# One ring of row tiles, tables with alternating ranks, deviations by logarithm and exponential, and a new order of steps in a graph attention kernel

## The chip, the cores and the metric

The kernel runs on one core of a Trainium2 chip. The metric is the device time of one execution in microseconds (us); for several executions the median is given. The core has a matrix engine (TensorE, PE in the profile), a vector engine (VectorE, DVE), an engine for activation functions (ScalarE, ACT), a general one (GpSimd, POOL) and a queue engine (SyncE, SP). Transfers between the memory of the chip and the on-chip memory run on DMA engines, and are started by SP, ACT and POOL.

## What is computed

`x` has 32 batches of 512 rows (channels) by 1024 columns (nodes); `adj` is 512 by 512. Two layers follow each other, each on a layer norm of the rows with a ReLU:

```python
h = jnp.maximum(_layernorm(x, axis=-1), 0.0)
q = jnp.einsum('c,bcn->bn', wq, h)
k = jnp.einsum('c,bcn->bn', wk, h)
scores = q[:, None, :] + k[:, :, None]
scores = jnp.where(scores > 0, scores, 0.01 * scores)
att = softmax(scores, axis=-1)
agg = jnp.einsum('bcn,bmn->bcm', h, att)
x = x + relu(jnp.einsum('oc,bcm->bom', adj, agg) + bm[None, :, None])

h = jnp.maximum(_layernorm(x, axis=-1), 0.0)
W = adj * adj
x = x + jnp.einsum('bnf,nm->bmf', h, W) + bias
```

The attention has 1024 by 1024 scores per batch, each a leaky ReLU of a sum of two numbers. For a fixed node m, the sum q[n] + k[m] is positive for all n whose q lies above -k[m] and negative for the others. If the nodes are sorted by q, then the softmax of a node is made of two parts: a sum over the nodes of high rank with weights exp(q), and a sum over those of low rank with weights exp(0.01 q). So prefix sums over the sorted values, from both ends, replace the 1024 by 1024 matrix.

## The kernel before

**One batch.** A batch has 4 tiles of 128 channels by 1024 nodes (2 MB in all). `load` brings the tiles, `stats` (VectorE) makes mean and variance of each row, `norm` (ScalarE) the standard deviation, `slopes` (VectorE) its reciprocal, and `relu` (ScalarE) normalises in place. `scores` (TensorE) makes q and k in pieces of 256 nodes, `copy` brings them to the on-chip memory, and they go to a small table in the chip's memory and back as `row` (q of all nodes, on every partition). `columns` turns q and k so that each node has a partition (8 groups of 128 nodes). `factors` works out the maximum of q and the factors of a node.

**Ranks.** `rank` (VectorE) counts for each node how many q lie below its own; `lower` (ScalarE, a sign with a sum) counts how many lie below -k. `to_rows` and `from_rows` turn the two counts into row numbers of a table. `value` (TensorE, 32 matmuls of 128 by 512) multiplies h by the transposed adjacency, `spread` (ScalarE) copies the result out, and `scatter` (GpSimd, an indirect DMA of 128 rows) writes the values, 512 numbers and the node's q, into the rank's row of the table.

**Scan.** A table has 9 blocks of 126 ranks in 63 pairs. `fetch` (SP) reads a sorted table back in three pieces of three blocks; `weights` (ScalarE) makes the exponentials, `later`, `totals` and `stationary` (VectorE, TensorE, GpSimd) the triangular matrices, and `scan` (TensorE) the prefix sums, block after block, from both ends. Since the first row of each block takes what the block before it has summed, `sums` (ScalarE) copies one row into the next block, and copies the sums out, and SP writes them into the table, beside the sorted values: each row s of a table is three entries long (k = 0, 1, 2), of which `scan` fills 0 and 1 and `scatter` entry 2.

**Back.** `gather` (GpSimd, 8 indirect DMAs of 128 rows of three entries) reads for every node the two sums and the value at the border between them. `excess`, `divide`, `weigh` and `combine` (VectorE, ScalarE) make of them the attention's result. `turn` (TensorE) transposes it to channels by nodes and VectorE adds it to the tile that `reload` has read again from `x`. Then the second layer: `stats`, `norm`, `slopes`, `relu` into tiles of their own, `lift` (adds the bias), `propagate` (TensorE, 8 groups of 4 matmuls of 128 by 512) and `finish` (VectorE), which starts the write to `out` after a tile's second half.

**The order of the work.** There are no loops over batches in the usual sense. Each function is a step with a planned time in the dictionary `PLAN` (one for each call in a batch, in a unit of its own); a batch's steps stand `T = 80.647` later than the previous batch's. `FIRST` and `LAST` give the first five and the last five batches a shift, and a stretch about the mean of a step's times. `plan` puts all into one list, which is sorted by time and emitted once:

```python
t = s.b * T + t + shift + stretch * (t - mean)
...
steps.sort(key=lambda e: e[:2])
with tc.manual_schedule():
```

So the numbers set nothing but an order. Each engine executes its instructions in this order and each waits for what it needs; a step that stands early on its queue and waits holds up what stands behind it. SP's queue carries the loads, reloads, fetches, sums and outputs; ACT's the small table of q; POOL's the scatters and gathers. A batch lasts about five of these periods from load to output, so that several are in flight.

**Memory.** The tiles of 128 by 1024 come from three pools: `xp` (7 tiles), `yp` (7) and `hp` (4, the second layer's h). `load`, `reload` and `relu` choose between them. A pool hands out its tiles in turn, and one that is still read delays the step that wants it. The tables `td` are five in the chip's memory (`TABLES`), the batch number modulo five chooses one; `qd` are two. The values of a gather have one buffer (`gp`), the sorted blocks five (`vsp`), the scattered values eight (`vp`).

**Set-up.** Four small loads (`wq`, `wk`, `bm`, `bias`) and the adjacency; `turn_adjacency` transposes it on TensorE and `square` squares it on GpSimd. `pads` fills the rows of the tables that no rank has (zero, with q at -1e30), for all tables in one step.

Of the kernel before, what the change touches and what calls it, by code (L numbers as in the profile page):

```python
# [16 lines left out]
P = 128  # L17
# [8 lines left out]
TABLES = 5  # L26
PLAN = {
    "adjacency": (-108.2,),
    "biases": (103.637,),
    "columns": (-0.644,),  # L30
    "combine": (
        295.175, 296.981, 297.681, 298.56, 293.456, 294.898, 296.312, 299.441, 298.758,
        299.991, 297.356, 298.478, 299.289, 299.451, 296.18, 297.782,
    ),
    "compare_mask": (-39.924,),
    "divide": (279.776,),
    "excess": (274.084,),
    "factors": (31.052,),
    "fetch": (71.51,),
    "finish": (356.071, 361.635, 372.571, 377.123, 391.802, 417.732, 398.837, 420.531),  # L40
    "from_rows": (87.236,),
    "gather": (260.35, 264.453, 263.071, 264.447, 267.501, 263.458, 263.983, 262.344),
    "later": (82.669,),
    "lift": (343.707, 352.288, 361.264, 350.629),
    "load0": (-132.547,),
    "load1": (-83.561,),
    "load2": (-110.642,),
    "load3": (-58.45,),
    "lower": (25.135, 20.956, 15.44, 19.087, 14.733, 13.756, 46.166, 37.237),
    "masks": (-18.987,),  # L50
    "norm0": (-31.509,),
    "norm1": (326.35,),
    "pads": (-73.925,),
    "propagate": (346.423, 349.207, 352.169, 365.765, 371.233, 382.761, 381.981, 389.706),
    "rank": (17.984, 18.872, 20.129, 19.992, 25.594, 25.16, 26.367, 26.318),
    "reload0": (283.236,),
    "reload1": (289.947,),
    "reload2": (275.592,),
    "reload3": (294.126,),
    "relu0": (-21.389, -21.25, -20.652, -20.617),  # L60
    "relu1": (336.308, 336.463, 336.836, 338.53),
    "row": (1.149,),
    "scan": (88.672, 94.082, 102.974, 119.344, 135.342, 151.67, 171.394, 183.726, 197.836),
    "scatter": (49.236, 49.927, 49.759, 49.383, 53.226, 50.436, 50.301, 52.611),
    "scores": (-2.312,),
    "slopes0": (-23.106,),
    "slopes1": (327.104,),
    "spread": (10.418, 15.798, 4.081, 13.981, 26.765, 25.953, 18.654, 18.733),
    "square": (58.25,),
    "stationary": (82.87, 113.617, 158.362),  # L70
    "stats0": (-66.042, -57.278, -62.987, -37.25),
# [725 lines left out]
```

## Time and profile before

| | |
|---|---|
| median of 3 runs | 2368.5 us (2366.38 to 2370.43) |
| span of the profiled execution | 2372.9 us |
| mean granted TensorE clock | 0.987 of full speed |
| moved by DMA | 643.45 MB, mean 271 GB/s |
| VectorE's statistics | 256 of 677 ns in layer 0, 256 of 668 ns in layer 1 |
| ScalarE's ReLU, layer 0 | 128 of 1231 ns |
| scatter, gather on GpSimd | 256 of 1064 ns, 256 of 951 ns |

The profile is of one execution. Its page gives each engine's busy time, the span in 40 slices with busy tenths (9 is 90% or more) and the granted TensorE clock, the DMA queues, the chain of work that ended last, and groups of instructions (source line L, engine, operation, result<-operands, count, mean duration). The trace behind it can be asked for the chain in order of time (start, length, engine, what), for an engine's instructions with the idle time ahead of them, and for the busy time of every engine in a given stretch. In these answers `pv` is the value product, `pg` the propagate product, `sc` a scan, `tr` a turn, `pq` scores, `pr` columns, `pd` totals, `td` a table, `vs` a sorted piece, `g` the gathered rows, `h` the second layer's normalised tiles.

### The profile page before, as it was taken

The numbers are of one execution on the slowest core, as the hardware profiler recorded it, in microseconds if no ns is written. First come the engines' busy times: TensorE is split into PE (matmuls) and PEld (weight loads), VectorE is DVE, ScalarE is ACT, GpSimd is POOL, SyncE is SP. The second block draws the span as 40 slices with busy tenths as digits, with TensorE's granted clock in tenths as the row PEclk, the third lists the DMA queues.
The fourth block names the chain that finished last, engine by engine and source line by source line (L and its number), as shares of the span: only waits on it lengthen the run. The fifth ranks groups of instructions, "written<-read, shape, count | busy, mean of one in ns | idle before, by whom it ended". The sixth has DMA issues, their size and how long they took to land.

```text
span 2372.9 us, 28069 instructions
## 1 busy us (share of the span) xinstructions
PE 2295.2 (97%) x7568; PEld 1011.5 (43%) x7568; DVE 1952.6 (82%) x5008; ACT 1599.8 (67%) x2880; POOL 720.7 (30%) x973
## 2 busy tenths in 40 slices
PE   7787999999999999999999999999999999999997
PEld 3233444444444444444444444444444444443443
DVE  7457888888888888888888888888888888888875
ACT  4576776766777766777676777676677676677551
POOL 2233333233333233233223233323333323233310
PEclk9988999999999999999999999999999999999998
DMA  6678888989999998999999999899988898998972
GB/s 222 171 181 277 284 284 277 296 269 276 287 290 285 296 286 266 277 299 283 288 292 266 276 294 287 287 291 272 268 291 276 288 302 253 276 282 269 311 294 79
DMA packets 206894, 643.45 MB, mean 271 GB/s; under 512 B 29120, under 2 KB 29248, under 8 KB 206736
## 3 DMA queue, kind: packets, MB, share of 16 engines
q1 hardware_dynamic: 142944, 355.74, 53.9%
q0 software_dynamic: 57344, 268.99, 30.7%
q10 hardware_dynamic: 6448, 16.92, 2.3%
q8 instruction: 61, 1.00, 0.2%
q14 instruction: 97, 0.79, 0.1%
HBM read 429.94 MB, written 211.60 MB: 270 GB/s over the span
## 4 chain that ended last, share of the span: by engine, by line
PE 85%; DMA 5%; DVE 5%; ACT 2%; issue 1%; POOL 1%; SPq 0%; ACTq 0%; another core or an unknown queue 0%; POOLq 0%; DVEq 0%
PE pg L703 34%; PE pv L550 33%; PE sc L639 10%; PE tr L696 4%; DMA vs<-td 2%; PE pq L445 2%; PE sc L636 1%; DVE g L689 1%; DVE st L414 1%; DMA g<-td,idg 1%; DMA td<-v,idx 1%; DVE junk L492 1%; ACT x L433 0%; DVE junk L487 0%; DMA x<-in_x_dram 0%
## 5 line engine op out<-in xcount | busy, mean ns | idle before, releaser
L703 PE MATMUL pg<-h,wsq 128*128 128x512 f32 x2048 | 911.2, 598 | 12.8 <-ACT h L433 12.8
L550 PE MATMUL pv<-wmT,x 128*128 128x512 f32 x2048 | 908.8, 598 | 5.9 <-ACT x L433 4.4
L703 PEld LDWEIGHTS pg<-h,wsq 128*128 128x128 f32 x2048 | 382.8, 191 | 517.4 <-issue 476.1
L550 PEld LDWEIGHTS pv<-wmT,x 128*128 128x128 f32 x2048 | 382.0, 191 | 499.1 <-issue 452.6
L623 POOL TENSOR_TENSOR sm<-mask_a,wc 128x192 f32<-128x192 f32 x96 | 51.9, 540 | 1254.9 <-DVE wc L600 785.7
L689 DVE SCALAR_TENSOR_TENSOR g<-g,cf 128x512 f32<-128x512 f32 x512 | 357.9, 756 | 46.4 <-ACT g L685 44.3
L648 ACT COPY vs<-sc 1x512 f32<-1x512 f32 x256 | 145.3, 567 | 272.9 <-PE sc L639 208.6
L563 POOL DMA_INDIRECT td<-v,idx x256 | 272.4, 1064 | 149.3 <-POOL v L562 36.3
L639 PE MATMUL sc<-vs,sm 128*64 128x512 f32 x1024 | 282.6, 621 | 21.3 <-POOL sm L623 11.1
L503 ACT ACTIVATE junk<-qrow,qk 128x1024 bf16<-128x1024 f32 x256 | 294.0, 1148 | 5.5 <-DMA qrow<-qd 2.5
L660 POOL DMA_INDIRECT g<-td,idg x256 | 243.5, 951 | 147.4 <-issue 71.5
L698 DVE SCALAR_TENSOR_TENSOR y<-tr,nbm,y 128x512 f32<-128x512 f32 x256 | 174.4, 744 | 66.3 <-PE tr L696 61.2
L711 DVE SCALAR_TENSOR_TENSOR y<-pg,bm_sb,y 128x512 f32<-128x512 f32 x256 | 185.8, 731 | 32.4 <-PE pg L703 32.0
L651 ACT COPY t<-sc 128x512 f32<-128x512 f32 x288 | 168.0, 583 | 40.7 <-DMA td<-t 35.3
L433 ACT ACTIVATE x<-x,nmr,rstd 128x1024 f32<-128x1024 f32 x128 | 148.6, 1231 | 64.9 <-DVE nmr L425 64.9
L492 DVE TENSOR_SCALAR_CACHE_REDUCE junk<-qrow,qk,cnt 128x896 bf16<-128x896 f32 (+6 forms) x224 | 180.5, 806 | 8.2
L685 ACT ACTIVATE g<-g,cf 128x512 f32<-128x512 f32 x256 | 167.7, 712 | 6.4 <-DVE cf L679 5.3
L487 DVE TENSOR_SCALAR_CACHE_REDUCE junk<-qrow,qk 128x128 bf16<-128x128 f32 (+6 forms) x224 | 166.0, 741 | 6.6
L414 DVE BATCH_NORM_STATS2 st<-x 128x6 f32<-128x512 f32 x256 | 162.7, 677 | 9.6 <-DMA x<-in_x_dram 9.6
L439 DVE TENSOR_TENSOR y<-y,bias_sb 128x1024 f32<-128x1024 f32 x128 | 154.3, 1219 | 16.0 <-ACT h L433 16.0
L557 ACT COPY v<-pv 128x512 f32<-128x512 f32 x256 | 141.8, 579 | 29.7 <-PE pv L550 14.0
L414 DVE BATCH_NORM_STATS2 st<-y 128x6 f32<-128x512 f32 x256 | 160.4, 668 | 0.0
(111 smaller groups left out, 1923.1 us busy)
## 6 DMA issues: line engine op xcount, KB each, us to landing
vs<-td SPq DMA_DIRECT2D x192, 384.8 KB
td<-t SPq DMA_DIRECT2D x576, 128.2 KB
x<-in_x_dram SPq DMA_DIRECT2D x128, 512.0 KB
y<-in_x_dram SPq DMA_DIRECT2D x128, 512.0 KB
out_dram<-y SPq DMA_DIRECT2D x128, 512.0 KB
qrow<-qd ACTq DMA_DIRECT2D x32, 512.0 KB
td<-v,idx POOLq DMA_INDIRECT x256, 8.3
g<-td,idg POOLq DMA_INDIRECT x256, 13.8
```

The lines of the kernel that those rows point to most:

```text
L414: nc.vector.bn_stats(st[:, i, :], s.x[c][:, ts(i, HALF)])
L492: nc.vector.tensor_scalar(junk[:, j * P :], s.qrow[:, j * P :], qc, first, ALU.is_lt, ALU.add, accum_out=s.cnt[:, 1, j : j + 1],)
L503: nc.scalar.activation(junk, s.qrow, AF.Sign, bias=s.qk[:, 1, j : j + 1], accum_out=s.sgn[:, j : j + 1])
L550: nc.tensor.matmul(pv, s.h[c][:, ts(j, P)], wmT[:, c, :], start=(c == 0), stop=(c == NC - 1))
L563: i = nc.gpsimd.indirect_dma_start(tds[s.b % TABLES][:, :], bass.IndirectOffsetOnAxis(ap=s.idx[j // 4][:, j % 4 : j % 4 + 1], axis=0), v[: ...
L639: nc.tensor.matmul(p[ts(k, HP), :], m[:, k, :], s.vs[h][:, 0:C], start=True, stop=True)
L651: nc.scalar.copy(t[:, 0:C], p)
L660: nc.gpsimd.indirect_dma_start(s.g[:, j, :], None, tds[s.b % TABLES][0 : 3 * NB * HP, :].rearrange("(s k) w -> s (k w)", k=3), bass.Indire ...
L689: nc.vector.scalar_tensor_tensor(r, s.g[:, j, k * W : k * W + C], s.cf[:, k, j : j + 1], r, ALU.mult, ALU.add)
L698: nc.vector.scalar_tensor_tensor(xh, pt, nbm[:, o : o + 1], xh, ALU.max, ALU.add)
L703: nc.tensor.matmul(pg, wsq[:, r, ts(c, P)], s.h[r][:, ts(i, HALF)], start=(r == 0), stop=(r == NC - 1),)
L711: nc.vector.scalar_tensor_tensor(xh, s.pg.pop((c, i)), bm_sb[:, c : c + 1], xh, ALU.add, ALU.add)
```

## The change

1. The pools `xp`, `yp` and `hp` become one ring of 18 tiles (`ROWS`), and `load`, `reload` and `relu` take the next tile of it without a choice.
2. There are six tables instead of five, and four small tables for q instead of two (`QROWS`).
3. The layout of a table changes. Before, even ranks stood in the first half of the table and odd ranks in the second, 64 rows for each block. Now each block has 128 rows, even ranks in the first 64 and odd ranks in the last 64. So `fetch` reads three blocks as one transfer over 128 partitions instead of two over 64, and `to_rows`, `from_rows`, `sums` and `gather` reckon the row numbers anew; `from_rows` has one small VectorE operation more. `gather` now has the whole table as its source. A new step, `holes`, one for each table, fills entries 0 and 1 of the rows of odd ranks with zeros (2.36 MB each: 64 rows of 9 blocks of 1026 numbers), by a fill on GpSimd and a transfer on SP. `pads` is a step for each table, with three transfers instead of four.
4. `norm` no longer takes a square root. It takes the logarithm of the variance plus epsilon and the exponential of minus half of that, and `slopes` improves this with one Newton step of three small VectorE operations in place of the reciprocal. The table of activation functions is chosen once at the start.
5. All numbers of `PLAN`, `FIRST` and `LAST` are new, with the same period `T`; `FIRST` and `LAST` have six batches each instead of five, and nearly every stretch is now different from zero.

```diff
-TABLES = 5
+TABLES = 6
+ROWS = 18
+QROWS = 4
 PLAN = {
...
-    "fetch": (71.51,),
+    "fetch": (55.702,),
...
-    "load0": (-132.547,),
-    "load1": (-83.561,),
-    "load2": (-110.642,),
-    "load3": (-58.45,),
+    "load0": (-118.054,),
+    "load1": (-95.975,),
+    "load2": (-139.732,),
+    "load3": (-67.716,),
...
-    "scores": (-2.312,),
+    "scores": (-17.953,),
...
-    "turn0": (305.575, 305.673, 305.631, 305.894),
+    "turn0": (289.134, 289.42, 289.067, 289.284),
...
 FIRST = {
...
     "rank": (
-        (-28.589, 0.7379), (-2.87, -0.0721), (-9.055, 1.3394), (2.403, 0.1874), (-13.459, 0.0458),
...
+        (-34.203, 1.1418), (-6.053, 1.4966), (-21.016, 1.0747), (1.116, -0.688), (10.257, 0.0895),
+        (-0.536, -1.144),
+    ),
...
-    xp = ctx.enter_context(tc.tile_pool(name="xp", bufs=7))
-    yp = ctx.enter_context(tc.tile_pool(name="yp", bufs=7))
-    hp = ctx.enter_context(tc.tile_pool(name="hp", bufs=NC))
+    xp = ctx.enter_context(tc.tile_pool(name="xp", bufs=ROWS))
...
     def sorted_rows(td, h, n):
-        rows = td.rearrange("(o h s k) w -> o s h k w", o=2, s=HP, k=3)
-        return rows[:, :, h : h + n, 2, :]
+        rows = td.rearrange("(h p k) w -> p h k w", p=P, k=3)
+        return rows[:, h : h + n, 2, :]
...
-    root = const.tile([P, 1], F32, name="root")
-    nc.scalar.activation(root, eps_sb, AF.Sqrt)
+    nc.scalar.preload_act_table_set("natural_log_exp_and_others")
...
-    def pads(s):
-        pad = vp.tile([P, W], F32, tag="v", name="pad")
+    def pads(s, i):
+        pad = vp.tile([P, W], F32, tag="v", name=f"pad_{i}")
         nc.vector.memset(pad, 0.0)
         nc.vector.memset(pad[:, C : C + 1], FAR)
-        for td in tds:
-            for o in range(2):
-                nc.sync.dma_start(sorted_rows(td, 0, NB - 1)[o, 0], pad[0 : NB - 1, :])
-                nc.sync.dma_start(sorted_rows(td, NB - 1, 1)[o, :, 0], pad[0:HP, :])
+        for o in range(2):
+            nc.sync.dma_start(sorted_rows(tds[i], 0, NB - 1)[o * HP], pad[0 : NB - 1, :])
+        nc.sync.dma_start(sorted_rows(tds[i], NB - 1, 1)[:, 0], pad)
+
+    def holes(s, i):
+        rows = tds[i].rearrange("(h o s k) w -> o s h (k w)", o=2, s=HP, k=3)
+        z = vsp.tile([P, 3, W], F32, tag="vs", name=f"z_{i}").rearrange("p k w -> p (k w)")
+        nc.gpsimd.memset(z[0:HP, 0 : 2 * W], 0.0)
+        nc.sync.dma_start(
+            rows[1, :, :, 0 : 2 * W],
+            z[0:HP, 0 : 2 * W].unsqueeze(1).broadcast_to([HP, NB, 2 * W]),
+        )
...
     def load(s, c):
-        pool, tag = (yp, "y") if NC <= s.b * NC + c < NC + 7 else (xp, "x")
-        t = pool.tile([P, N], F32, tag=tag, name=f"x_{s.b}_{c}")
+        t = xp.tile([P, N], F32, tag="x", name=f"x_{s.b}_{c}")
...
-        nc.scalar.activation(s.std, s.mv[:, :, 1], AF.Sqrt, bias=eps_sb)
+        nc.scalar.activation(s.std, s.mv[:, :, 1], AF.Ln, bias=eps_sb)
+        s.rstd = sp.tile([P, NC], F32, tag=f"rstd{layer}", name=f"rstd{layer}_{s.b}")
+        nc.scalar.activation(s.rstd, s.std, AF.Exp, scale=-0.5)
...
     def slopes(s, layer):
-        s.rstd = sp.tile([P, NC], F32, tag=f"rstd{layer}", name=f"rstd{layer}_{s.b}")
-        nc.vector.reciprocal(s.rstd, s.std)
+        t = sp.tile([P, NC], F32, tag=f"step{layer}", name=f"step{layer}_{s.b}")
+        nc.vector.scalar_tensor_tensor(t, s.mv[:, :, 1], EPS, s.rstd, ALU.add, ALU.mult)
+        nc.vector.scalar_tensor_tensor(t, t, -0.5, s.rstd, ALU.mult, ALU.mult)
+        nc.vector.scalar_tensor_tensor(s.rstd, t, 1.5, s.rstd, ALU.add, ALU.mult)
...
         if layer == 1:
-            pool, tag = (xp, "x") if s.b == B - 2 else (hp, "h")
-            h = pool.tile([P, N], F32, tag=tag, name=f"h_{s.b}_{c}")
+            h = xp.tile([P, N], F32, tag="x", name=f"h_{s.b}_{c}")
...
-        odd = 3.0 * NB * HP
+        odd = 3.0 * HP
...
-        nc.vector.scalar_tensor_tensor(s.idg, pair, 1.0, block, ALU.add, ALU.add)
+        nc.vector.tensor_scalar(block, block, float(P - PAIRS), 1.0, ALU.mult, ALU.add)
+        nc.vector.tensor_tensor(s.idg, pair, block, ALU.add)
...
-            for o in range(2):
-                d = nc.sync.dma_start(t[ts(o, HP)], sorted_rows(tds[s.b % TABLES], 3 * i, 3)[o])
-                for k in s.sc:
-                    tc.add_manual_dep(d.ins, k.name, DONE, reason="any of them may hold a row")
+            d = nc.sync.dma_start(t, sorted_rows(tds[s.b % TABLES], 3 * i, 3))
+            for k in s.sc:
+                tc.add_manual_dep(d.ins, k.name, DONE, reason="any of them may hold a row")
...
-        nc.sync.dma_start(td[ts(ha, HP), 0, :], t[0:HP, :])
-        nc.sync.dma_start(td[ts(hb, HP), 1, :], t[HP:P, :])
+        nc.sync.dma_start(td[ts(2 * ha, HP), 0, :], t[0:HP, :])
+        nc.sync.dma_start(td[ts(2 * hb, HP), 1, :], t[HP:P, :])
...
-            tds[s.b % TABLES][0 : 3 * NB * HP, :].rearrange("(s k) w -> s (k w)", k=3),
+            tds[s.b % TABLES].rearrange("(s k) w -> s (k w)", k=3),
```

## The prediction

> **What bounds the kernel now.** I read the page's busy shares and slices first, then the chain of waits, then busy time by stretch, then the chain again in the first 262 us, last TensorE's own timeline at the end.
>
> ```profile
> span 2372.9 us, 28069 instructions
> PE 2295.2 (97%) x7568; PEld 1011.5 (43%) x7568; DVE 1952.6 (82%) x5008; ACT 1599.8 (67%) x2880; POOL 720.7 (30%) x973
> PE   7787999999999999999999999999999999999997
> DMA  6678888989999998999999999899988898998972
> ```
>
> The first four slices (240 us) and the last are the only ones in which PE is not full. The chain of waits over the whole span:
>
> ```profile
> 525.43 17.36 PE pv L550 x40
> ...
> 595.96 17.36 PE pv L550 x40
> ...
> 666.48 17.36 PE pv L550 x40
> ```
>
> The same piece returns every 70.53 us, batch after batch: the middle is PE's own work and nothing else. 32 x 70.53 = 2257 of 2373 us; some 116 us are filling and draining. By stretch (columns: length, then busy us of PE, PEld, DVE, ACT, POOL; granted clock, DMA share, GB/s):
>
> ```profile
> 0.00:60.00 60.00, 44.54 (x163) 19.13 (x164) 43.20 (x132) 29.46 (x44) 15.43 (x29) 1.00 0.70 221
> 60.00:120.00 60.00, 47.20 (x146) 18.09 (x145) 26.71 (x92) 35.01 (x72) 13.27 (x24) 0.95 0.67 172
> 120.00:180.00 60.00, 53.46 (x168) 21.45 (x165) 32.06 (x110) 42.01 (x84) 19.17 (x29) 0.91 0.74 185
> 180.00:240.00 60.00, 42.16 (x157) 19.19 (x155) 41.48 (x121) 40.33 (x79) 19.01 (x25) 0.86 0.85 265
> 480.00:900.00 420.00, 420.00 (x1410) 186.64 (x1409) 363.10 (x930) 296.92 (x536) 133.38 (x177) 1.00 0.92 283
> ```
>
> PE idles 52.6 us in the first 240, and its clock falls after the waits. What it waits for, from the chain of the first 262 us:
>
> ```profile
> 96.79 7.00 DMA td<-v,idx
> ...
> 107.26 9.96 DMA vs<-td
> ...
> 180.13 16.16 DMA g<-td,idg
> ...
> 224.42 11.12 DMA vs<-td
> ```
>
> Each early batch goes rank, scatter to the table, fetch, weights, scan in series. At the end (PE's timeline, idle time in brackets):
>
> ```profile
> 2141.28 0.44 PE L461 MATMUL pr<-ident,qr 128*128 128x128 f32 x2 [2.53 <-ACT qr L450]
> ...
> 2212.05 0.28 PE L612 MATMUL pd<-w,mask_a 128*64 128x9 f32 x2 [2.12 <-ACT w L589]
> ...
> 2337.72 30.41 PE L703 MATMUL pg<-h,wsq 128*128 128x512 f32 x64 [10.29 <-ACT h L433]
> ```
>
> **The Trainium skill.** "ScalarE: Activation LUTs", What ACT_TABLE_LOAD costs, puts a table load at 1283 ns; the trace agrees (61 at std, 28, 27 and 6 at the exponentials, 1283 ns each). Its Table sets section says that one set holds both exponential and logarithm; the built program has one load left. "TensorE: Matmul & The Clock Gate", The HAM clock gate: an idle PE restarts at half clock. The trace agrees: four scan matmuls take 2.43 us after the 4.39 us wait at 118.58, and 1.08 warm. "DMA: Bandwidth & Descriptors", Issuing engines are not separate DMA queues: all transfers share 16 engines, so the new zero fills compete with whatever flies beside them; most that I see here is 405 GB/s (10 to 15 us).
>
> **The change, part by part.**
> *Table loads.* 122 x 1.283 = 157 us leave ACT, 64 exponentials x 0.30 = 19 come. DVE gets per norm three products for one reciprocal (+2 x 0.17) and one more small operation in from_rows: +0.85 us per batch. In the middle both are hidden under PE: per 70.53 us DVE has 9.5 us free, ACT 20. Worth 0 there; without that cover it would be -4.3 and +0.85 us per batch.
> *One ring.* 7 + 7 + 4 tiles become 18: the same memory. PE's work per batch is untouched (same 4336 matmuls). *Fetch* is 3 transfers instead of 6 of the same bytes: 3 x 0.62 us of SP issue less in each batch's chain.
> *New times, middle.* In the built order a batch still turns three batches, propagates four batches behind its scores. From excess to the turn DVE has about 25 us (lifts, two statistics, factors, divide, 16 combines of 0.70) under 27 us of PE work; the gathers follow stationary0 as before (8.4 us into the period), so land before excess. I take 0; a stall of 0.1 us per batch would cost 3.
> *New times, start.* This is the cost. SP now issues first the adjacency (1 MB), three pads and a tile of the third batch; the first batch's last two tiles stand behind the wait for the bias vector. Such waits for small loads held SP to 9.82 and 13.35 us in the trace, at the second batch's tiles; now they meet the first batch. I take issue at 12 us and 4 us to land: first statistics at 16 (4.78 before). Then 4 x 1.45, pad and masks on DVE, two activations and four small products: 24.5; four relus 4.64 and the last three score groups: scores end at 32 (17.96 before). The row of q came 6.5 us later; now it flies beside three zero fills of 2.36 MB (7.1 MB, 17.5 us of all engines at 405 GB/s), so 6.5 to 14; I take 9.5: 42 (24.9 before). A rank costs 538.8/256 = 2.10 us; eight, two pad fills, factors (1.9) and one to_rows (1.4): first scatter at 64, eight at 1.46 and a fill on POOL: last at 77 (49.5 before). Fetch 3.5 later, weights 12 after that: 92.5, against 67.5.
> Second batch: its ranks stand on DVE behind those weights, after two statistics (3.0); last scatter 30 us later, fetch 6.5, landing 12.5, weights 1.3: 142 (117.6). Third: only five ranks are left behind (10.5 + 3.0 + 1.4), eight scatters, then the same: 188 (170). Then stationary0 and, queued behind it on POOL, the first batch's gathers: 1.3 + 25.1 (171.35 to 196.41), and 16.4 of excess, divide, weigh and combine: the first turn at 231 (214.15).
> PE has 145.6 us of work in front of that turn (146.5 before), so it runs 85.5 us behind its work, against 67.6. But before, it went on losing, to 76.1 at the first propagate (263.34, 187.2 us of work in front), since the fourth batch's scan waited; now that scan comes at about 252, when PE gets there. Loss: 86 - 76 = **+10**, bounds +1 (bias vector at 8 us, row at 6.5, faster fetch) to +18.
> *New times, end.* The copy of q now stands ahead of the previous batch's weights on ACT, and PE has 7 us of work between scores and columns instead of 3.5: the 2.53 and the cold restart behind it (1.7) go. The last fetch starts with three issues and the last totals wait about 1 instead of 2.4. With the one gather buffer, turns chain: from the 29th batch's turn to the end of the 30th's took 44.0 us, since one of eight gathers stood behind stationary0 of the last batch, itself behind its weights; now all eight go first, 10.3 issue, 14 landing, 2 divide, 13 to combine, turn: 40.3. The two later links stay 39 and 45. Sum -4.2 - 0.3 - 3.7 = **-8**, bounds -12 and -3.
> *Last chain.* Logarithm, exponential and three products in the last norm for square root and reciprocal, all bare: +0.30 + 0.05 + 2 x 0.19 = **+0.7**. The table loads there were already hidden.
> Sum: +10 - 8 + 0.7 = +2.7 on the span, 2375.6. The profiled execution is 4.4 above the median of the runs, 2368.5; on the median that makes 2371, and I say 2370.
>
> **Rivals.** *Slower: the late start is not repaid.* Place: the third batch's weights. The first propagate's lag is their time + 42.7 - 145.6, so from 179 us on every microsecond is paid. If the fills hold row, scatter and fetch up by 5 us more, and the chain of turns keeps its 44 us, it is +15 - 4 + 1: 2380. For it: DMA is already 0.67 to 0.85 busy in that stretch. Against: the fills' 14.2 MB are spread, two of six come later. *Faster: the end counts, the start doesn't.* If small loads land at 8 us without the first batch's tiles beside them, and fetches as 3 transfers save 2 us in each of three links, weights are in at 179: 2361. *A new period:* if the relieved ACT shortened a batch by 1 us it would be -28; against it, PE is busy 420.00 of 420. If instead the new order stalls PE by 0.5 us a batch, +14. *The change does nothing* where it says it does: that is so for ring and table loads in the middle, and is in the forecast.
>
> **How the numbers follow.** A measurement of this kernel tells 0.2% (4.7 us) from no change. Even, within that: 0.32. Late start not repaid 0.28, new stalls in the middle 0.07: slower 0.35. Faster end with a cheap start 0.32, a shorter period 0.01: 0.33. Even and the two rivals beside it rest on two terms of opposite sign, each known to some 8 us, so none of the three is far ahead. The likeliest alone spans 2364 to 2373; the range takes the outer bounds of both terms, -10 (+1 - 12 + 0.7) to +16 (+18 - 3 + 0.7), on 2368.5, and 3 us for the middle on either side: 2355 to 2387.
>
> **What would show it.** Right: pieces still 70.53 us apart; first scores past 28 us, third batch's weights at 183 to 193, first propagate PE 80 to 90 us behind; no 2.5 us wait at the last columns, the last norm's gap near 11; ACT some 138 us less busy with the same span. Wrong if the first batch's tiles land before 10 us, if PE shows waits between 300 and 2000 us, or if the last three turns take the 129 us they took (2198.45 to 2327.4).

## The result

The changed kernel takes 2386.96 us (median of 4 runs, 2383.59 to 2390.99), the kernel before 2367.44 us beside it (2366.37 to 2370.43). The ratio is 1.0077, with a 95% interval of 1.0061 to 1.0092: slower by 19.5 us. The forecast of 2370 with no difference to be told was not met; the time lies at the very upper edge of the range of 2355 to 2387, beyond the 2380 of the rival "the late start is not repaid".

The page of the changed kernel, its span, busy shares and slices:

```profile
span 2385.6 us, 28030 instructions
PE 2283.3 (96%) x7568; PEld 1004.8 (42%) x7568; DVE 1986.7 (83%) x5178; ACT 1438.8 (60%) x2821; POOL 705.6 (30%) x979
PE   5578999999999999999999999999999999999997
DMA  9868888888888878888888888888878888878881
```

ScalarE is 161 us less busy (138 were worked out), and the span is longer all the same. The loss sits in the first three slices (some 60 us each): TensorE is busy for 5, 5 and 7 tenths where the kernel before had 7, 7 and 8. In the first two slices the DMA engines are at 9 and 8 tenths instead of 6 and 6.

Busy time by stretch of the changed kernel (length, then busy us of PE, PEld, DVE, ACT, POOL; granted clock, DMA share, GB/s):

```profile
0.00:60.00 60.00, 35.99 (x140) 17.24 (x141) 34.30 (x115) 26.22 (x41) 9.30 (x18) 0.83 0.90 242
60.00:120.00 60.00, 34.77 (x89) 14.87 (x87) 10.77 (x36) 9.50 (x25) 13.39 (x22) 0.80 0.86 245
120.00:180.00 60.00, 42.98 (x125) 15.73 (x123) 44.68 (x163) 44.35 (x91) 14.49 (x25) 0.72 0.65 176
180.00:240.00 60.00, 51.90 (x167) 20.22 (x165) 30.18 (x109) 41.52 (x86) 20.83 (x32) 0.96 0.88 296
480.00:900.00 420.00, 419.99 (x1412) 185.49 (x1412) 370.60 (x966) 267.41 (x528) 127.22 (x178) 1.00 0.83 279
```

In 240 us PE is busy for 165.6 (187.4 before). Between 60 and 120 us VectorE does 10.8 us of work and ScalarE 9.5: they wait for transfers. The middle is full, as before, but it is not the same. The chain of waits in the middle of the changed kernel:

```profile
921.23 10.30 PE pg L900 x24
...
991.46 10.30 PE pg L900 x24
...
1061.68 10.30 PE pg L900 x24
```

The piece returns every 70.22 us; in the kernel before it was every 70.53. The prediction had given a shorter period one chance in a hundred.

With TensorE's timelines side by side, the two profiled executions (2372.9 and 2385.6 us) compare as follows. "Behind" is the difference of the same event.

| event | before | changed | behind |
|---|---|---|---|
| first propagate | 263.3 | 289.0 | +25.6 |
| scores of the seventh batch | 367.6 | 393.6 | +26.0 |
| scores of the 28th batch | 1849.2 | 1868.9 | +19.8 |
| first transpose of the last turn | 2323.8 | 2334.5 | +10.8 |
| start of the last propagate | 2337.7 | 2351.4 | +13.7 |
| end of the span | 2372.9 | 2385.6 | +12.7 |

So the start costs 26, the middle gives back 6, the end 9, the last norm takes 3, and the last propagate with the output gives back 1. That is 12.7 of the 19.5 us between the medians. The other 7 come from which execution was profiled: with the 1.7 us that lie around a span, that of the kernel before makes 2374.6, near the top of its runs (2361.67 to 2374.92 in 38 later ones), while the changed kernel's is at its median. A second profile of the kernel before, below, lies near the top as well, so where its median runs save these 7 us is not seen.

**Where the start goes.** The chain of waits of the changed kernel, from the end of the first batch's ranks:

```profile
55.98 0.38 ACT qr L645
56.38 8.98 DMA qd<-qr
65.43 11.73 DMA qrow<-qd
77.23 0.29 SPq L551
77.56 0.30 SPq L551
77.90 0.34 SPq L552
78.34 0.29 SPq L551
78.67 0.46 DMA td<-pad
79.21 1.19 POOL td L761
...
90.55 12.69 DMA td<-v,idx
103.39 0.39 SPq L777
103.83 0.48 SPq L777
104.35 9.27 DMA vs<-td
```

The first batch's scatter (L761) comes at 79.2, though its row numbers were ready at 60.1: the timeline of the vector engine and that of GpSimd.

```profile
59.93 0.16 DVE L724 SCALAR_TENSOR_TENSOR idx<-blockq,rk 128x4 uint32<-128x4 f32 x1
```

```profile
79.21 1.19 POOL L761 DMA_INDIRECT td<-v,idx  x1 [39.04 <-DMA td<-pad]
```

It waits for the small fills of its own table (`pads`, L551 and L552). By the numbers of `pads` the first table's fills come fourth of six. In SyncE's queue (SPq) the fourth group is the one issued from 56.6 us:

```profile
34.07 4.09 SPq L558 DMA_DIRECT2D td<-z  x3
38.21 11.67 SPq L593 DMA_DIRECT2D x<-in_x_dram  x2
56.59 2.72 SPq L551 DMA_DIRECT2D td<-pad  x2
60.37 1.37 SPq L552 DMA_DIRECT2D td<-pad  x1
...
77.23 0.63 SPq L551 DMA_DIRECT2D td<-pad  x2
```

The fills at 77.2 and later, which the chain above names, belong to other tables: the releaser there is inferred, and SP's wait ahead of them, 11.4 us for the second batch's row of q, does not bear on this scatter. The trace's completion events show the fourth group landing at 77.6, 77.8 and 78.3 us, some 17 us after its last issue. What lies between are the three zero fills issued from 34.1 us. Their packets fly from 37.1 to 71.0, and between 43 and 70 us SP's queue moves no other data; two tiles of `x` and then the small fills follow. And the zero fills are slow: between 42 and 70 us the DMA engines are 0.99 busy at 203 GB/s, while between 10 and 14 us, with tiles of `x`, they moved 397 GB/s. Why a fill runs at half the rate is not shown.

### The profile page after: what moved, and what is told of

It is laid out like the page before. It is cut to its first block, busy times and chain, and to the rows that moved or that the text cites. A ratio compares the mean times of both kernels' runs of the same rounds, so it can differ in the third digit from the quotient of the medians.

```text
span 2385.6 us, 28030 instructions
## 1 busy us (share of the span) xinstructions
PE 2283.3 (96%) x7568; PEld 1004.8 (42%) x7568; DVE 1986.7 (83%) x5178; ACT 1438.8 (60%) x2821; POOL 705.6 (30%) x979
## 4 chain that ended last, share of the span: by engine, by line
PE 81%; DVE 9%; DMA 6%; ACT 2%; issue 2%; POOL 1%; SPq 0%; ACTq 0%; DVEq 0%; POOLq 0%
PE pg L900 33%; PE pv L748 31%; PE sc L836 9%; PE tr L893 4%; PE pq L640 2%; DVE g L886 2%; DMA vs<-td 2%; DVE st L606 1%; DVE junk L687 1%; PE sc L833 1%; DVE junk L682 1%; DMA td<-t 1%; DMA td<-v,idx 1%; DMA x<-in_x_dram 1%; DVE y L908 1%
## 5 line engine op out<-in xcount | busy, mean ns | idle before, releaser
L748 PE MATMUL pv<-wmT,x 128*128 128x512 f32 x2048 | 918.6, 600 | 0.9 <-DVE qk L661 0.9
L761 POOL DMA_INDIRECT td<-v,idx x256 | 281.6, 1100 | 244.7 <-POOL v L760 45.0
L836 PE MATMUL sc<-vs,sm 128*64 128x512 f32 x1024 | 267.4, 621 | 9.6 <-issue 4.8
L908 DVE SCALAR_TENSOR_TENSOR y<-pg,bm_sb,y 128x512 f32<-128x512 f32 x256 | 183.8, 736 | 31.5 <-PE pg L900 31.2
L687 DVE TENSOR_SCALAR_CACHE_REDUCE junk<-qrow,qk,cnt 128x640 bf16<-128x640 f32 (+6 forms) x224 | 180.5, 806 | 8.2
L848 ACT COPY t<-sc 128x512 f32<-128x512 f32 x288 | 168.1, 584 | 31.5 <-DMA td<-t 21.6
L682 DVE TENSOR_SCALAR_CACHE_REDUCE junk<-qrow,qk 128x384 bf16<-128x384 f32 (+6 forms) x224 | 165.3, 738 | 14.7 <-DMA qrow<-qd 9.7
L882 ACT ACTIVATE g<-g,cf 128x512 f32<-128x512 f32 x256 | 160.9, 710 | 6.5 <-DVE dn L874 3.3
L628 ACT ACTIVATE h<-y,nmr,rstd 128x1024 f32<-128x1024 f32 x128 | 153.0, 1237 | 6.2 <-DVE nmr L621 3.1
```

The lines of the kernel that those rows point to most:

```text
L682: nc.vector.tensor_scalar(junk[:, 0 : j * P], s.qrow[:, 0 : j * P], qc, None, ALU.is_le, ALU.add, accum_out=s.cnt[:, 0, j : j + 1],)
L687: nc.vector.tensor_scalar(junk[:, j * P :], s.qrow[:, j * P :], qc, first, ALU.is_lt, ALU.add, accum_out=s.cnt[:, 1, j : j + 1],)
L748: nc.tensor.matmul(pv, s.h[c][:, ts(j, P)], wmT[:, c, :], start=(c == 0), stop=(c == NC - 1))
L761: i = nc.gpsimd.indirect_dma_start(tds[s.b % TABLES][:, :], bass.IndirectOffsetOnAxis(ap=s.idx[j // 4][:, j % 4 : j % 4 + 1], axis=0), v[: ...
L836: nc.tensor.matmul(p[ts(k, HP), :], m[:, k, :], s.vs[h][:, 0:C], start=True, stop=True)
L908: nc.vector.scalar_tensor_tensor(xh, s.pg.pop((c, i)), bm_sb[:, c : c + 1], xh, ALU.add, ALU.add)
```

## The experiments

The ratios are to runs of the kernel before on the same chip. Chips differ: the kernel before has a median of 2367.5 us on that of runs 1 to 4, 2372.4 on that of runs 5 to 8, 2370.7 for 9 to 11 and 2368.3 for 12, so times of different groups are compared by ratio. "First propagate" is when TensorE starts the first propagate product, counted from the start of the span. "Six fetches" and "three fetches" are the transfers in which a batch's sorted table is read back.

| run | edit | median us | ratio (95%) | first propagate |
|---|---|---|---|---|
| changed | | 2387.0 | 1.0077 (1.0061 to 1.0092) | 289.0 |
| 1 | changed, first table's small fill early | 2380.0 | 1.0048 (1.0034 to 1.0062) | 281.8 |
| 2 | changed code, old order, zero fills spread | 2402.0 | 1.0148 (1.0132 to 1.0163) | 292.4 |
| 3 | before, second scan later | 2363.6 | 0.9978 (0.9971 to 0.9985) | 258.3 |
| 4 | before, norm by logarithm | 2371.7 | 1.0021 (1.0013 to 1.0028) | 263.4 |
| 5 | changed, old table layout, six fetches, no zero fills | 2393.6 | 1.0091 (1.0078 to 1.0104) | 278.5 |
| 6 | 5 with small fill early, last ReLUs in order | 2388.5 | 1.0063 (1.0051 to 1.0075) | 280.0 |
| 7 | old layout, old start, new rest | 2372.5 | 1.0000 (0.9990 to 1.0011) | 264.5 |
| 8 | before again | 2373.0 | 1.0003 (0.9995 to 1.0011) | 263.0 |
| 9 | before, three fetches, no zero fills | 2349.5 | 0.9909 (0.9895 to 0.9922) | 245.2 |
| 10 | 9 and 3 | 2346.0 | 0.9898 (0.9882 to 0.9913) | 244.4 |
| 11 | changed, three fetches, no zero fills, and the edits of 6 | 2357.1 | 0.9943 (0.9929 to 0.9957) | 264.6 |
| 12 | changed code, old order, three fetches, no zero fills | 2349.7 | 0.9919 (0.9902 to 0.9936) | 242.6 |

### The first four: fill, order, period, norm

Run 1, the order of the tables in `pads`:

```diff
-    "pads": (-13.323, 30.141, -95.948, 9.602, -266.549, -158.167),
+    "pads": (-266.549, -158.167, -95.948, 9.602, -13.323, 30.141),
```

> The changed kernel, with the fill of the first table's rows without a rank put at the place where the fifth table's stood, and the others in turn; as many fills and transfers as before at the same places. Theory A, the start is late because the first scatter, whose row numbers are ready at 60, waits until 79.2 us for this small fill, which stands on SP behind a wait for the second batch's row of q: first scatter at 61, first turn at 228 instead of 245.5, median 2370 us. Rival, the zero fills' traffic is what makes the start late: the scatter starts earlier, but rows, scatters and fetch take longer, the first turn comes no earlier than 240 and the median stays above 2382.

The scatter starts at 61.7, as theory A had it, but of its 18 us only 7 arrive at the first propagate. (The wait for the row of q, theory A's reason, stands ahead of other tables' fills, as shown above; the first table's waited behind the zero fills.) The chain of waits of run 1:

```profile
61.73 1.18 POOL td L761
...
64.88 14.08 DMA td<-v,idx
...
80.41 7.58 DMA td<-v,idx
...
91.13 13.37 DMA vs<-td
```

A scattered block takes 14 us to land (7.00 in the chain of the kernel before, for the second batch), the fetch 13.4. So the late small fill is worth 7 us, and something else holds the transfers up; the rival has a part.

Run 2, the dictionaries of the kernel before put into the changed kernel, with times of my own for the zero fills and their zeros in a tile of the scattered values' pool, in two transfers each (the two main edits):

```diff
-    "holes": (-87.013, -69.157, -60.895, 39.922, 68.519, -167.733),
+    "holes": (-74.5, 55.0, 140.0, 225.0, 305.0, 398.0),
...
-        z = vsp.tile([P, 3, W], F32, tag="vs", name=f"z_{i}").rearrange("p k w -> p (k w)")
+        z = vp.tile([P, W], F32, tag="v", name=f"z_{i}")
```

> All functions of the changed kernel (ring, six tables, alternating ranks, logarithm and exponential), in the order of the kernel before; only the six zero fills, which that order has no place for, are spread over the first 400 planned us, and their zeros come from tiles of the scattered values' pool in two transfers each. Theory A, the order makes the whole difference: start and middle as before (pieces 70.53 us apart, first propagate at 262 to 266), the gap ahead of the last propagate 10.9 us for 10.29, median 2367 to 2371. Rival, the code costs time by its zero fills: first propagate past 270, median above 2376. Second rival, the code gains time since ScalarE is relieved: pieces 70.2 us apart, median 2359.

Theory A fell here: the code in the old order is slower than in the new one. The chain of waits of run 2 shows the three first fetches:

```profile
65.09 19.01 DMA vs<-td
...
122.32 14.73 DMA vs<-td
...
181.93 19.95 DMA vs<-td
```

In the kernel before, the second fetch has 9.96 in this place and the fourth 11.12. In run 2 SP issues a zero fill at 58.8, 113.8 and 175.5, right ahead of the three, on the same queue. The pieces are 70.53 us apart, though, with all of the new code: the period belongs to the order.

Run 3:

```diff
-    "scan": (88.672, 94.082, 102.974, 119.344, 135.342, 151.67, 171.394, 183.726, 197.836),
+    "scan": (88.672, 95.5, 102.974, 119.344, 135.342, 151.67, 171.394, 183.726, 197.836),
```

> The kernel before, with one planned time changed: the second scan of a batch moves from 94.082 to 95.5, so that a value product stands between it and the first, as in the changed kernel. Theory A, the period of 70.53 us holds a hidden wait of 0.5 us, the third of three scans in a row waiting for ScalarE's copy of a row, and 0.15 to 0.2 us for one more alternation come back: pieces 70.2 us apart, median 2358 to 2359. Rival, the shorter period of the changed kernel comes from the relieved ScalarE: pieces 70.5 to 70.7 us apart, median 2367 to 2373.

The period is 70.22 us: the hidden wait was real. It can be seen in the kernel before, but not in the matmuls. TensorE's timeline and that of its weight loads, kernel before:

```profile
945.15 3.43 PE L639 MATMUL sc<-vs,sm 128*64 128x512 f32 x12
```

```profile
946.91 0.19 PEld L639 LDWEIGHTS sc<-vs,sm 128*64 128x64 f32 x2 [0.72 <-ACT vs L648]
```

Twelve scan matmuls in a row (one step each of two batches, then the first one's next) seem to run without a gap; but the weight loads of the steps ahead of it are 0.28 us apart, and here it is 0.72, with ScalarE's copy of a row (L648) as the releaser. In the chain of waits four scan matmuls take 1.01 us, eight 1.87, twelve 3.28: the last four cost 1.41 where the second four cost 0.86. The changed kernel puts a value product between them: its scans take 0.51 us less in a period and the propagate 0.20 less, the value products 0.41 more. The 420.00 us busy of 420 had looked like proof that nothing waits, and they were not.

The medians differ by 3.9 us instead of 9: 28 periods of 0.30 make 8.4. Some of it is lost again: from the 28th to the last batch's scores this kernel takes 286.1 us for 284.0, with waits of 0.5 and 1.0 us between 1975 and 1998. But the two profiled spans differ by 10.3 us (2362.6, 2372.9), so what the medians lack is about the distance by which the profile of the kernel before lies above its median.

Run 4, `norm` and `slopes` of the changed kernel in the kernel before (the diff is that of the change's fourth part).

> The kernel before, with the norm alone taken from the changed one (logarithm, exponential, Newton step, one table of functions). Theory A, ScalarE's table loads were hidden: some 138 us less busy on ScalarE, pieces 70.53 us apart, the gap ahead of the last propagate 10.9 us, median 2366 to 2370. Rival, the table loads set the period: pieces 70.2 us apart, median 2359.

The period is 70.53, the gap ahead of the last propagate 10.90 (10.29): the table loads were hidden and the Newton step costs 0.6 us at the end, as worked out. The median is 4.2 us higher (0.13 to 0.28%), though the profile of run 4 is 1.3 us shorter than that of the kernel before and shows the same start and end within 2 us. So here, too, the profile of the kernel before stands 5.5 us higher than its median would have it; where these come from was not settled.

### The next four: zero fills against six fetches

Theory B, that the zero fills make most of the start, was to be shown with the old layout. Run 5 undoes `sorted_rows`, `pads`' transfers, `holes`, the index arithmetic, `fetch`, `sums` and `gather`; its core:

```diff
-        rows = td.rearrange("(h p k) w -> p h k w", p=P, k=3)
-        return rows[:, h : h + n, 2, :]
+        rows = td.rearrange("(o h s k) w -> o s h k w", o=2, s=HP, k=3)
+        return rows[:, :, h : h + n, 2, :]
...
-            plan(s, holes, "holes")
...
-            d = nc.sync.dma_start(t, sorted_rows(tds[s.b % TABLES], 3 * i, 3))
+            for o in range(2):
+                d = nc.sync.dma_start(t[ts(o, HP)], sorted_rows(tds[s.b % TABLES], 3 * i, 3)[o])
```

> The changed kernel with its own order, but with the layout of the tables before: even ranks in the first half, odd ranks in the second, a piece fetched in two transfers, and so no zero fills. Theory B, formed after the fill order gave back 7 us only and the old order with the zero fills cost 34: the 14.2 MB of zero fills beside the first batches' loads, scatters and fetches are the larger part of the late start. It expects the first propagate at 270 (between 266 and 275) instead of 289, and a median of 2365 to 2372. Rival, theory A as it stood, the late start comes from SP's queue and its waits: first propagate past 281, median above 2379.

The first propagate is 10 us earlier (278.5), less than theory B said and more than its rival; yet the whole run is no faster (1.0091, where the changed kernel has 1.0077 and the intervals overlap), and the expected median was missed by over 20 us. The first table's small fills are issued at 56.7, in the same place as in the changed kernel, and the first scatter starts at 62.0: without zero fills ahead of them they are not late. The scores of the eighth batch come 8 us before the changed kernel's, those of the tenth 4, and the last batch's 4 after. Something that the layout had given was gone; the last four runs show that it was the three fetches.

Run 6 adds two edits, the order of `pads` as in run 1 and

```diff
-            plan(s, relu, f"relu{l}", l)
+            plan(s, relu, f"relu{l}", l, args=((2,), (3,), (1,), (0,)) if l and s.b == B - 1 else None)
```

> The run before with two more edits: the first table's small fill at the early place, and the last batch's four ReLUs in the order of their channels, so that the first matmul of the last propagate waits for one of them and not for three. Theories A and B together: another 7 us at the start (first propagate at 263), the gap ahead of the last propagate 10.9 us instead of 13.18, median 2356 to 2362. Rival, the small fill was late only because the zero fills held the queue: no gain at the start, median 2363 to 2370.

The small fill's place gives nothing at the start without the zero fills (280.0). So run 1's 7 us are a joint effect of the two: the small fill was late only behind zero fills. The median of 2388.5 misses theory and rival alike. The gap ahead of the last propagate is 10.92. In the changed kernel it was 13.18; TensorE's and ScalarE's timeline at its end:

```profile
2351.38 29.72 PE L900 MATMUL pg<-h,wsq 128*128 128x512 f32 x64 [13.18 <-ACT h L628]
```

```profile
2347.82 4.64 ACT L628 ACTIVATE h<-y,nmr,rstd 128x1024 f32<-128x1024 f32 x4 [0.87 <-DVE nmr L621]
```

The new times of `relu1` (327.187, 327.488, 326.943, 326.159 for the four channels) make the order 3, 2, 0, 1; the last batch's stretch of 4.78 only spreads it. The first matmul wants channel 0: two ReLUs of 1.16 us too many stand ahead of it.

In run 7 the first 650 steps stand in the old order and the remaining ones in the new, with the old layout and the last ReLUs in order (the core of the edit):

```diff
+    steps.sort(key=lambda e: (e[4], e[1]))
+    head = steps[0:650]
+    tail = sorted(steps[650:], key=lambda e: e[:2])
```

> Old layout without zero fills; the first 650 steps in the order of the kernel before, all others in the order of the changed kernel, the last ReLUs in the order of their channels. If the start alone made the changed kernel slower: start as before (first propagate at 263), pieces 70.22 us apart, no wait of 2.5 us at the last columns, gap 10.9 us: before less 7 in the middle less 8 at the end plus 0.6, a median of 2352 to 2356. Rival, what is gained in the middle is lost again in the chain of the last turns: 2358 to 2366.

The start is the old one (264.5 to the first propagate), though ring, norm and six tables are the new ones: these cost the start 1 us at most. The period is 70.22. Nevertheless the run ends where the kernel before does, and the expected 2352 to 2356 were missed. From the last scores to the last turn it takes 190.5 us; the changed kernel takes 186.0 in the same order. Run 8 is the kernel before again.

> The kernel before without any edit, for a second profile of it: its first profiled execution lies some 5 us above the median of its runs, and the profiles of the changed kernels don't. Expected: pieces 70.53 us apart again, a span of 2364 to 2368, and the difference in the first 300 us or in the last 250, where the engines wait.

The expected span of 2364 to 2368 was missed: it is 2376.7, again near the top of the runs on its chip (2367.22 to 2379.02). The first propagate is at 263.0, the period 70.53; waits of 2.43 us at the last columns and 2.99 at the last totals are there again, and 192.3 us lie between the last scores and the last turn (190.6 in the first profile).

### The last four: three fetches without zero fills

Runs 1 and 2 have 185.6 and 185.3 us from the last scores to the last turn, the changed kernel 186.0; runs 3 to 8, all with six fetches, 189.1 to 192.3. That points to the fetches, not to the order. A third layout has them without anything to fill: even ranks in the first half as before, but a partition's nine rows beside each other, so that all 128 partitions have one stride. Row numbers are 9 times the place in the block plus the block. Run 9 makes these edits, among others, in the kernel before (`pads` also makes three transfers for each table instead of four):

```diff
-        rows = td.rearrange("(o h s k) w -> o s h k w", o=2, s=HP, k=3)
-        return rows[:, :, h : h + n, 2, :]
+        rows = td.rearrange("(p h k) w -> p h k w", p=P, k=3)
+        return rows[:, h : h + n, 2, :]
...
-        nc.vector.tensor_scalar(rk, rk, odd, 5.0, ALU.mult, ALU.add)
-        nc.vector.scalar_tensor_tensor(rk, pair, 3.0 - 2.0 * odd, rk, ALU.mult, ALU.add)
+        nc.vector.tensor_scalar(rk, rk, odd, 3.0 * NB + 2.0, ALU.mult, ALU.add)
+        nc.vector.scalar_tensor_tensor(rk, pair, 3.0 * NB - 2.0 * odd, rk, ALU.mult, ALU.add)
...
-        nc.vector.scalar_tensor_tensor(s.idx[i], block, 3.0, rk, ALU.mult, ALU.add)
+        nc.vector.scalar_tensor_tensor(
+            s.idx[i], block, 3.0 * (1 - NB * PAIRS), rk, ALU.mult, ALU.add
+        )
...
-            for o in range(2):
-                d = nc.sync.dma_start(t[ts(o, HP)], sorted_rows(tds[s.b % TABLES], 3 * i, 3)[o])
+            d = nc.sync.dma_start(t, sorted_rows(tds[s.b % TABLES], 3 * i, 3))
...
-        nc.sync.dma_start(td[ts(ha, HP), 0, :], t[0:HP, :])
-        nc.sync.dma_start(td[ts(hb, HP), 1, :], t[HP:P, :])
+        nc.sync.dma_start(td[0:HP, ha, 0, :], t[0:HP, :])
+        nc.sync.dma_start(td[0:HP, hb, 1, :], t[HP:P, :])
```

> The kernel before, in its own order, with a third layout of the tables: all even ranks in the first half as before, but the nine rows that one partition holds beside each other. So a piece is fetched in one transfer over 128 partitions as in the changed kernel, gathers still read the first half alone, and nothing has to be filled with zeros. One small operation more in from_rows. Theory C: what the changed kernel gains at its end comes from the three fetches, since the run of its code in the old order took 185.3 us from the last scores to the last turn as well, and the runs with six fetches took 189 to 192. It expects 185 to 187 from the last scores to the last turn, 3 to 5 us less at the start, pieces 70.53 us apart, and a ratio of 0.995 to 0.998. Rival, the gain at the end is the new order's: 190 to 192 us there, and a ratio of 0.999 to 1.002.

Twice as much as theory C said: 21 us. From the last scores to the last turn 184.8 us, and the waits at the last columns and totals are gone, in the old order. And the start is 18 us earlier, not 3 to 5. SP's timeline of the kernel before, and of run 9, at the fourth batch's fetch:

```profile
220.25 4.79 SPq L580 DMA_DIRECT2D vs<-td  x6
```

```profile
207.43 1.45 SPq L584 DMA_DIRECT2D vs<-td  x3
```

ScalarE's timeline at the weights of the same fetch, the last piece, before and in run 9:

```profile
235.62 0.30 ACT L589 ACTIVATE w<-vs,nq 128x3 f32<-128x3 f32 x1 [4.43 <-DMA vs<-td]
```

```profile
217.75 0.28 ACT L593 ACTIVATE w<-vs,nq 128x3 f32<-128x3 f32 x1
```

From the first issue to the last piece's weights it is 15.4 us before and 10.3 in run 9. The same link was 15.5 and 11.7 for the first batch, 13.4 and 9.9 for the second, 13.5 and 10.4 for the third: 15.5 us together, in four links that follow each other. The issue makes 2.5 to 3.3 of each. The prediction had counted 1.9, three issues of 0.62. In run 9 the last weights do not even wait for the fetch (no idle time stands ahead of them). Places of rows and `pads` changed with the fetches, but 15.5 of the 18 us lie in these links.

Run 10 moves the second scan as in run 3.

> The run before with the second scan of a batch one value product later. If the two gains add: pieces 70.22 us apart, a ratio of 0.991 to 0.995, the fastest so far. Rival, the later scan takes back at the end what it gives in the middle, as it seems to have done in part alone (ratio 0.9978 where the period alone would make 0.9965): 0.995 to 0.998.

The best of all, 24.7 us below the kernel before. The later scan gives 3.5 us, about as much as alone (3.9 in run 3) and less than its period would make: the period is 70.22, but a wait of 1.70 us for a tile of `sums` comes at 1961.

Run 11 is the changed kernel with this layout and the edits of run 6.

> The changed kernel in its own order with the third layout, so with three fetches and no zero fills, with the first table's small fill early and the last ReLUs in the order of their channels. What is then left of the late start is the order of loads and steps alone. Theory B: against the run with the small fill early alone (ratio 1.0048, first propagate at 281.8), the zero fills' 10 us and the last ReLUs' 2.3 go: first propagate at 270 to 275, 185 us from the last scores to the last turn, gap 10.9, ratio 0.998 to 1.001. Rival, the order alone makes the late start: first propagate at 279 to 282, ratio 1.003 or more.

It beats both kernels, and by more than expected (0.9943). Between it and run 1 lie the zero fills, the places of the rows and the last ReLUs: 17.1 us at the first propagate (264.6, 281.8), 1% in all. The second batch's two small transfers of q, which ScalarE issues, land 3.3 and 4.2 us after their issue; in the changed kernel, beside the zero fills of SP's queue, it was 9.0 and 11.7. Run 6 differs from run 11 in the six fetches and the places of the rows: its span is 30.2 us longer (2388.2, 2358.0), 15.4 of it at the first propagate. Run 12 is run 2 with this layout.

> All functions of the changed kernel in the order of the kernel before, as in the second run, but with the third layout and so without zero fills. It differs from that run in the fills and the rows' places alone. If the fills are what made that run slow: first propagate at 244 to 248 as in the kernel before with three fetches, instead of 292, and a ratio of 0.991 to 0.994, 0.002 above that kernel for the logarithm's longer norm. Rival, ring, tables or norm cost more in that order: first propagate past 255, ratio above 0.997.

So it came. In the old order, with the places that I had given them, the zero fills cost 49.8 us at the first propagate (292.4, 242.6); ring, tables and norm cost that start nothing. Runs 11 and 12 also set the two orders side by side, with three fetches and no zero fills in both: the new order reaches the first propagate 22 us later and ends 11.5 us later (spans 2358.0, 2346.5), so what it gains in the middle does not repay its start.

## Why the prediction was right and wrong

The forecast was a time of 2370 and no difference. What came is the first half of the rival "the late start is not repaid", and more of it: the fills hold row, scatter and fetch up. Its other half did not come, since the chain of turns did not keep its 44 us. That the time still lies in the range is luck: the start cost 16 us more than forecast, and a middle forecast at nothing gave back 6. Of the signs that the prediction had named, the late first scores and the missing wait at the last columns came; the period of 70.53, the third batch's weights at 183 to 193 and a gap near 11 us did not.

The first propagate, taken apart by these runs, starting from 263.3 us:

| part | us | from runs |
|---|---|---|
| three fetches for six | -18.1 | 9 against before |
| the new order of the start (with ring, tables and norm) | +19.4 | 11 against 9 |
| zero fills | +17.1 | 1 against 11 |
| the first table's small fill behind them | +7.2 | changed against 1 |
| sum: 289.0 | +25.6 | |

Taken in another sequence the parts shift a little: with six fetches the new order costs 16.7 (run 6 against before), and in the new order three fetches give 15.4 (11 against 6). So the order costs nearly as much as all the fills (24.3). Its part begins with the first batch's tiles, as the prediction had said: first statistics at 15.4 us in the changed kernel (predicted 16). Between runs 11 and 9 it is first scores at 26.1 instead of 13.3, and the first batch's last weights at 84.0 instead of 63.6.

- **The start, +10 predicted, +26 measured.** The failing term is the price of the 14.2 MB of zero fills: 3 us in the prediction (9.5 for the row of q instead of 6.5), 24.3 in the runs (17.1 and 7.2). The prediction priced only those beside that row, at 405 GB/s; they flew at 203 with the DMA engines 0.99 busy, so three fills took 34 us (37.1 to 71.0) and not 17.5. And it left out what stands behind them on SP's queue: the small fills that the first scatter waits for, at 79.2 where 64 was predicted. What the prediction had cited from the Trainium skill, "DMA: Bandwidth & Descriptors", Issuing engines are not separate DMA queues, held, and more strongly than it was used: ScalarE's transfers of q slowed down beside SP's fills (9.0 and 11.7 us for 3.3 and 4.2 in run 11). The first scores (31.5 us, predicted 32) and the row (by 40.0 us, predicted 42) were right. From the first scatter on, all times are late by about as much: weights of the third batch 207 (188), first turn 244 (231).
- **Fetch, worked out as 3 x 0.62 us in each link.** The runs show 3 to 5 us in each of four links. This error and that of the fills have opposite signs, so the sum of the start missed by 16 and not by more.
- **The middle, 0 predicted, -6 measured.** The step "PE is busy 420.00 of 420" took a busy TensorE for one without waits. Run 3 shows that the third of three scan steps in a row waited half a microsecond, in most of the batches, in the time counted as busy.
- **The end, -8 predicted, -9 measured.** The size was right, and of the reasons one. The chain of turns got shorter as predicted: the 30th batch's link takes 39.6 us (44.0 before, 40.3 predicted), the last three turns 123.8 (128.8 before). The order does most of that: with six fetches in the new order (runs 5 to 7) the link takes 41.2 to 41.4 and the three turns 125.1 to 125.3. But these runs lose it ahead of the turns, 67.6 to 68.8 us from the last scores to the end of the 29th batch's turn (65.4 before). The waits at the last columns and totals vanish with three fetches in the old order as well (runs 9 and 12), so they are not the order's alone.
- **The last chain, +0.7 predicted, +2.9 measured.** The norm's part is 0.6, as run 4 shows. The rest is the order of the last four ReLUs, which the new times turned round (run 6); the prediction had looked at the order of functions and not of the calls of one.
- **Table loads.** Hidden, as predicted: run 4 has the old period. (The prediction's 4336 matmuls are a slip without effect; both profiles count 7568.)

Two things are not settled. One is why both profiles of the kernel before lie near the top of its runs; against them the changed kernel, run 3 and run 4 all come out 5 to 7 us better by profile than by median. The other is why the zero fills moved at half the rate of the loads.

## What to carry over

A fill of memory that seems to cost nothing, because nothing waits for it, is paid by the serial transfers beside and behind it: at a start where every step waits for a transfer, here with 24 us in one order and 50 in another. Take its rate from a stretch in which it flies, and follow each small transfer that a critical step depends on through its queue, to its landing and not only to its issue. And where an engine is "busy" all the time, look at the gaps between its weight loads and at the length of like groups before taking its period as its work: here three short steps in a row hid half a microsecond in most of the batches, of which 0.3 could be had.

## What was not expected of the hardware

One transfer over 128 partitions instead of two over 64 of the same bytes, three times in a row, shortened the time from the first issue to the last piece's weights from 15.4 to 10.3 us: 3.3 us of this are the issues on SP (4.79 and 1.45). Zero fills moved 203 GB/s with the DMA engines 0.99 busy, where loads of `x` moved 397; and small transfers issued on the same queue behind them landed 17 us and more after their issue. With a zero fill issued just ahead on the same queue, fetches took 15 to 20 us (run 2; 10 and 11 in the kernel before). And TensorE's matmul records can follow each other without a gap across a wait of half a microsecond; the wait shows in the weight loads.
